# A four-image mixer kernel: first image loaded ahead of the setup, the operands' sums and more weighing on GpSimd, tanh left in PSUM, reciprocals a step later

## The chip, the cores and the metric

The kernel runs on one core of one Trainium2 chip. A core has TensorE (PE, matrix products into PSUM), VectorE (DVE), ScalarE (ACT) and GpSimd (POOL), each with a queue worked off in order, and a queue (SP) that only issues DMAs here. The metric is the device time of one launch in microseconds (us). All arithmetic is float32.

## The reference, cut to what matters

Four layers follow each other on x of shape (4, 128, 64, 64): 4 images, 128 channels, L = 4096 pixels. Each normalises its input in groups of 4 channels (`gn`) and adds its result to it.

```python
x = x + attention(gn(x))      # q, k, v by 128x128 matrices; softmax over all 4096 pixels; no heads
x = x + conv5x5(gn(x), c)     # c is gathered from small tables by index, c = tab_xx[i]*XX + tab_id[i]*identity
x = x + mamba(gn(x))          # below
x = x + conv3x3(gn(x), main_w)

def mamba(x):                 # 64 channels forward, 64 over the reversed pixels
    t  = Wx @ x + bx
    xt = silu(conv1d(t, 4 taps) + conv_b)
    delta = softplus(xt @ Wd + bd);  Bm = xt @ WB;  Cm = xt @ WC        # 64 states
    dA = exp(delta * A);  dBx = delta * xt * Bm;   A = -exp(Alog)
    h[l] = dA[l]*h[l-1] + dBx[l]                                        # for 128 channels x 64 states
    y = sum_over_states(h * Cm) + D * xt
    return Wp @ y + bp
```

## The kernel before

One program is written out by Python generators, so the order on each queue is the order in which these emit.

**The scan** (`scan_core`) is the long part: 128 channels x 64 states x 4096 steps per image, cut into 256 *ticks* of 128 rows (32 channels x 4 states) x 1024 steps, 1024 ticks in all. A chunk of 1024 steps lasts 64 ticks. A tick i is: `drive` on POOL (db = dx * b, L946), two `decay` on ACT (da = exp, into PSUM, L939), `recur` on DVE (the recurrence, two halves of 512, L956), weighing with the c row, either on DVE (L959, da in PSUM is one input) or in `weigh` on POOL (L977, both inputs in SBUF), and every second tick `collect` on PE (the sum over states, L991). `to_pool` (L899) says which: two ticks of five (i % 5 in 1, 3), and every third tick of the last image. In the loop at L1027 tick i emits the drive of i+2, the decay of i+1, recur i, weigh i-1, collect i-3 and the DMA loads of i+4 (`AHEAD`).

**The rest** (`images`, L1162) is emitted between the ticks: after each half tick the main loop (L1225) takes steps from the generator `work` until a credit of 1.4 is used up (`PACE` 2.8 per tick; 0.75 in the last image); a step returns its cost, 0.86 for a product of 512 columns, 0.7 for a `SLOT`. So while image b is scanned, image b+1 goes through attention (`attention`, 256 steps u of a score product, an exp and a value product each), the 5x5 convolution (`conv_pairs`) and the preparation of its scan (`scan_prep`, `scan_operands`). While the last image is scanned, the 3x3 convolutions of the others run. Image 0 has nothing to hide behind: its attention, convolution and half of its operands come before the first tick.

**The operands** (`scan_operands`) are laid out by hand over 51 slots. For tile i of 512 pixels, starting at slot 5i: the taps on PE into PSUM bank `s` (`taps`), in slot 5i+4 two ACT passes (`halves`, L783: half of it to xc; L785: tanh into an SBUF tile th), in slot 5i+5 `silu` on DVE (L789: xc = (th+1)*xc, two SBUF inputs), then three products (bank `a`, `z`, `s2`), softplus on ACT and `digits` on DVE. For each half of the image (HM = 4 tiles) slot 5(i+3)+15 takes the logarithms on ACT (`logs`), and then for each chunk of 1024: `join` (L823, DVE: delta += u, 512 wide, twice, both inputs in SBUF; DMA to `dd`), two slots later `drives` (L828, POOL: xc = delta * xc; DMA to `dxd`). When a half is through, `(b, i + HM)` is put in `ready`; `before(b)` (L1210), called ahead of the first loads of image b's scan, takes steps until the first half is ready.

**Attention's tail**: when block blk of 512 queries is through, `evict` copies acc; one step later `turn` brings the row sums onto the partitions (8 or 4 narrow PE products into bank `z`) and has DVE copy them (L494) and take the reciprocal (L496); two steps after that `settle` spreads the reciprocals (PE, bank `z`, L407) and DVE multiplies and adds (L504 to L506). For image 0 the row sums are gathered beside the attention by side sums of the exponentials (`side_sums`, L466 and L469: even steps DVE, odd POOL); for the others by PE (`sums`, L449, bank `z`).

**The start.** Constants are computed first from `wm` in the pool `early` (L102), which is closed at L205 after the tap weights `wtap` (L196). The pools of the large tiles are opened only in `program` (L1177), on the space that `early` gave back, and the first image is loaded into them. `build_conv_weights` (L218) gathers the 5x5 weights on DVE in 13 steps while image 0's attention begins; after each the main loop takes one step of attention (L1200).

Of the kernel before, what the change touches and what calls it, by code (L numbers as in the profile page):

```python
# [32 lines left out]
P = 128  # L33
# [19 lines left out]
def conv_preact_kernel(  # L53
# [45 lines left out]
    wv = const.tile([P, C], F32, name="wv")  # L99
    nc.scalar.dma_start(wv, mats[:, 2, :])  # L100
    setup = ExitStack()
    early = setup.enter_context(tc.tile_pool(name="early", bufs=1))  # L102
# [20 lines left out]
    def col(i):  # L123
        return vec[:, i : i + 1]
# [12 lines left out]
    a_neg = const.tile([P, NK * NQ], F32, name="a_neg")  # L137
    with tc.tile_pool(name="rates", bufs=1) as tmp:
        every = tmp.tile([P, NK, NQ, NI], F32, name="every")
        for k in range(NK):  # L140
            rates = vecs[k * SG : (k + 1) * SG, ALOG : ALOG + NST].unsqueeze(1)
            nc.scalar.dma_start(
                every[:, k].rearrange("p q j -> p (q j)"),
                rates.to_broadcast([SG, NI, NST]),
            )
        mine = tmp.tile([P, NI], F32, name="mine")
        nc.vector.tensor_reduce(
            mine, ident.rearrange("p (s i) -> p i s", i=NI), AX.X, ALU.add
        )
        every = every.rearrange("p k q i -> p (k q) i")  # L150
        mine = mine.unsqueeze(1).to_broadcast([P, NK * NQ, NI])
        nc.vector.tensor_tensor(every, every, mine, ALU.mult)
        nc.vector.tensor_reduce(a_neg, every, AX.X, ALU.add)
    nc.scalar.activation(a_neg, a_neg, AF.Exp)
    nc.vector.tensor_scalar(a_neg, a_neg, -1.0, None, ALU.mult)

    sel = const.tile([P, SG], F32, name="sel")
    nc.vector.tensor_reduce(
        sel, ident.rearrange("p (s i) -> p s i", i=NI), AX.X, ALU.add
    )  # L160
    skip = const.tile([P, P], F32, name="skip")
    nc.vector.tensor_scalar(skip, ident, col(DSKIP), None, ALU.mult)

# [26 lines left out]
    cbias = small.tile([P, 1], F32, tag="cbias", bufs=1, name="cbias")  # L190
    for k in range(KC):
        ptap = bank("saz"[k % 3], f"ptap{k}")[:, :C]
        nc.tensor.matmul(
            ptap, col(CONVW + k).to_broadcast([P, P]), ident, start=True, stop=True
        )
        nc.vector.tensor_tensor(wtap[:, k, :], wm[:, 3, :], ptap, ALU.mult)  # L196
    for t in range(KC - 1):

        nc.vector.tensor_reduce(
            edge[:, t : t + 1], vec[:, CONVW : CONVW + KC - 1 - t], AX.X, ALU.add  # L200
        )
    nc.vector.tensor_tensor(cbias, edge[:, 0:1], col(CONVW + KC - 1), ALU.add)
    nc.vector.scalar_tensor_tensor(cbias, cbias, col(BX), col(CONVB), ALU.mult, ALU.add)
    nc.vector.tensor_scalar(edge, edge, col(BX), -1.0, ALU.mult, ALU.mult)
    setup.close()  # L205
    hbias = const.tile([P, 1], F32, name="hbias")
    nc.vector.tensor_scalar(hbias, cbias, 0.5, None, ALU.mult)

# [161 lines left out]

    def attention(b, xs, xn, v, st, safe):
        ring = pools["big"].tile([P, NRING, MM], F32, tag="xt", name=f"pt_{b}")
# [107 lines left out]
        def turn(blk):  # L480

            raw, zs = state[blk]
            parts = [(zs, zsel)] if zs is not None else [
                (sides.pop((blk, e)), ones[:, 0:1]) for e in "dp"
            ]
            pz = bank("z", f"pz_{b}_{blk}")
            for t in range(TPM):
                for n, (part, add) in enumerate(parts):
                    nc.tensor.matmul(
                        pz[:, t : t + 1], part[:, bass.ts(t, P)], add,  # L490
                        start=n == 0, stop=n == len(parts) - 1,
                    )
            z = zall[:, b * NJT + blk * TPM : b * NJT + (blk + 1) * TPM]
            nc.vector.tensor_copy(z, pz[:, :TPM])  # L494
            zr = small.tile([P, TPM], F32, tag="zr", name=f"zr_{b}_{blk}")
            nc.vector.reciprocal(zr, z)  # L496
            state[blk] = raw, zr

        def settle(blk):
            raw, zr = state.pop(blk)  # L500
            pb = bank("z", f"pzb_{b}_{blk}")
            spread(pb, zr)
            cut = bass.ts(blk, MM)
            nc.vector.tensor_tensor(pb, raw, pb, ALU.mult)  # L504
            nc.vector.scalar_tensor_tensor(xs[:, cut], pb, bv_c, xs[:, cut], ALU.add, ALU.add)
            nc.vector.bn_stats(st[:, blk, :], xs[:, cut])  # L506
# [5 lines left out]
        for u in range(N + 2):  # L512
# [8 lines left out]
            if 0 <= w < N:  # L521
# [10 lines left out]
                if d == NJT - 1:  # L532
                    evict(blk - 1)
                    if blk < NM:
                        after(u, 1, turn, blk - 1)
                        after(u, 3, settle, blk - 1)
                    else:
                        turn(blk - 1)
                        yield PRODUCT
                        settle(blk - 1)  # L540
                        ready.add((b, "attended"))
                        break
# [3 lines left out]
            for f, args in later.pop(u, ()):  # L546
                f(*args)
                cost += PRODUCT
            yield cost or HOP
# [198 lines left out]
    def scan_operands(b, xn, mats4, piece):  # L748
# [3 lines left out]
        pad = KC - 1  # L752
        HM = NM // 2

# [25 lines left out]
        def halves(i):  # L780

            pt = pts.pop(i)
            nc.scalar.activation(xc[:, bass.ts(i, MM)], pt, AF.Identity, scale=0.5, bias=hbias)  # L783
            ths[i] = pools["bg"].tile([P, MM], F32, tag="w", bufs=4, name=f"th_{b}_{i}")
            nc.scalar.activation(ths[i], pt, AF.Tanh, scale=0.5, bias=hbias)  # L785
# [34 lines left out]
        def join(c):  # L820
            for i in range(c * CH // MM, (c + 1) * CH // MM):
                cut = bass.ts(i, MM)
                nc.vector.tensor_tensor(delta[:, cut], delta[:, cut], us.pop(i), ALU.add)  # L823
            nc.sync.dma_start(dd[c], delta[:, bass.ts(c, CH)])
# [19 lines left out]

        def logs(i):
            for n in range(i, i + HM):
                nc.scalar.activation(us[n], us[n], AF.Ln)
# [7 lines left out]
        for i in range(NM):  # L855
# [12 lines left out]
            at(t + 13, row, i, 2)  # L868
        for i in (0, HM):
            t = EVERY * (i + HM - 1) + 15  # L870
            at(t, logs, i)
            for n, c in enumerate(range(i * MM // CH, (i + HM) * MM // CH)):
                at(t + 1 + n, join, c)
                at(t + 3 + n, drives, c)
            at(t + 3 + HM * MM // CH, ready.add, (b, i + HM))
        at(1, piece, 1)
        at(2, piece, 2)
        at(2, ready.add, (b, "read"))
        at(EVERY * (NM - 1) + 4, ready.add, (b, "taps"))
        for t in range(max(slots) + 1):  # L880
            for f, args in slots.get(t, ()):
                f(*args)
            yield SLOT
        ready.add((b, "all"))

# [3 lines left out]
    def scan_core(mats4, ynds, before, widen, result):  # L889
# [7 lines left out]
        das = {}  # L897

        def to_pool(i):  # L899

            return i % 5 in (1, 3) if ticks[i][0] + 1 < B else i % 3 == 2

# [5 lines left out]
        def load(i):  # L908
            b, c, d, q, g = ticks[i]
            (bmat, cmat), dd, dxd, xcd, _ = mats4[b]  # L910
            if q == 0:
                for name, src in (("de", dd), ("dx", dxd)):
                    t = pools["rep"].tile([P, CH], F32, tag=name, name=f"{name}_{b}_{c}_{d}_{g}")
# [147 lines left out]
    def program(safe):  # L1061
# [22 lines left out]
        def front(b, xn, v):  # L1084

            xs = large(b + 1, f"xs_{b}")[:, :L]
            yield from load(xs, b)
            st = stats_tile(f"e{b}")
            yield from attention(b, xs, xn, v, st, safe)
            st2 = stats_tile(f"s{b}")  # L1090
# [85 lines left out]
        with ExitStack() as es, tc.manual_schedule():  # L1176
            pools["big"] = es.enter_context(tc.tile_pool(name=f"big{safe}", bufs=1))  # L1177
            pools["bg"] = es.enter_context(tc.tile_pool(name=f"bg{safe}", bufs=2))
            banks = ExitStack()
# [15 lines left out]
            if not safe:  # L1195
                with tc.tile_pool(name="fill", bufs=2) as pools["fill"]:
                    while not (0, "begun") in ready:
                        next(work)
                    with tc.tile_pool(name="tables", bufs=1) as tmp:
                        for _ in build_conv_weights(tmp):  # L1200
                            next(work)
                    while (0, "attended") not in ready:
                        next(work)
                del pools["fill"]
            pools["rep"] = es.enter_context(tc.tile_pool(name=f"rep{safe}", bufs=3))
            pools["rows"] = es.enter_context(tc.tile_pool(name=f"rows{safe}", bufs=3))
# [3 lines left out]
            def before(b):  # L1210

                nonlocal pace
                while (b, NM // 2) not in ready:
                    next(work)
# [24 lines left out]

    program(False)  # L1240


# [72 lines left out]
```

## Time and profile before

| | us |
|---|---|
| median of 3 runs | 4618.73 (4616.98 to 4622.92) |
| profiled execution | 4616.38 |
| its span, first to last instruction | 4613.4 |
| ahead of the first tick (first db) | 751.75 |
| image 0's ticks, up to image 1's first db | 986.2 |
| image 1's | 975.2 |
| image 2's | 976.5 |
| image 3's, to its last db | 832.4 |
| from there to the end | 91.3 |

| engine | busy us | share of the span |
|---|---|---|
| PE | 4058.3 | 88% |
| DVE | 3758.6 | 81% |
| POOL | 3561.4 | 77% |
| ACT | 2320.9 | 50% |

Shares of the whole span hide that the stages have different limits, so the profile is read by stretches: of each, how long every engine was busy. The clock granted to TensorE was 0.938 of full speed on the mean.

### The profile page before, as it was taken

The page shows a single profiled execution, that of the slowest core. Times are in us where ns is not written, and L with a number is a line of the kernel's source. Part 1 is how long each engine was busy: PE and PEld are TensorE (multiplying, and loading weights), DVE is VectorE, ACT ScalarE, POOL GpSimd, SP SyncE. Part 2 cuts the span into 40 slices and gives each one's busy share as a digit, 9 for nine tenths or more (in the row PEclk, how much of TensorE's full clock was granted, in tenths as well). Part 3 has the DMA queues.
Part 4 walks back from the last instruction along what each step waited for, and adds up shares of the span by engine and source line. Part 5 has one row for each costly group of instructions (what it writes and reads, how often), then busy time and mean ns, then how long its engine had stood idle before and what let it go on. Part 6 is the DMA issues. An engine that isn't in the chain of part 4 may idle for free. (4 is left out here: it accounts for less than half of the span.)

```text
span 4613.4 us, 43452 instructions
## 1 busy us (share of the span) xinstructions
PE 4058.3 (88%) x13568; PEld 1496.7 (32%) x13568; DVE 3758.6 (81%) x3672; ACT 2320.9 (50%) x4180; POOL 3561.4 (77%) x1684
## 2 busy tenths in 40 slices
PE   6999998999999978999999979999999658585767
PEld 3444443333333323333333333333333112121212
DVE  7222115989998989999999989999999999999993
ACT  2333206666665466666664476666554644444431
POOL 2333304889988968898989869899899699999992
PEclk9999998999999989999999989999999878787878
DMA  1000005454444446445444564544445565656561
GB/s 66 1 0 1 0 18 214 171 166 169 169 171 157 171 182 217 158 170 177 171 167 157 200 219 171 173 174 167 162 163 180 205 233 201 220 206 220 196 228 44
DMA packets 210577, 719.47 MB, mean 156 GB/s; under 512 B 24864, under 2 KB 25760, under 8 KB 210208
## 3 DMA queue, kind: packets, MB, share of 16 engines
q1 hardware_dynamic: 208736, 715.87, 44.3%
q8 instruction: 109, 1.79, 0.2%
q14 instruction: 132, 1.08, 0.1%
q10 hardware_dynamic: 1600, 0.73, 0.1%
HBM read 649.07 MB, written 67.44 MB: 155 GB/s over the span
## 5 line engine op out<-in xcount | busy, mean ns | idle before, releaser
L946 POOL TENSOR_TENSOR db<-dx,br 128x1024 f32<-128x1024 f32 x1024 | 2403.9, 2367 | 339.0 <-DVE hc L956 75.7
L939 ACT ACTIVATE da<-de,a_neg 128x512 f32<-128x512 f32 (+1 forms) x1793 | 1343.5, 752 | 1011.0 <-DVE da L956 690.8
L415 PE MATMUL sc<-r,x 128*128 128x512 f32 x2048 | 1090.3, 615 | 53.5 <-ACT last L972 23.4
L427 PE MATMUL acc<-pt,v 128*128 128x512 f32 x2048 | 1050.1, 595 | 1.7
L977 POOL TENSOR_TENSOR hc<-hc,cr 128x1024 f32<-128x1024 f32 x392 | 929.1, 2370 | 11.4 <-ACT last L972 8.5
L991 PE MATMUL y<-hc,sel 128*32 128x512 f32 x4096 | 674.1, 654 | 279.6 <-POOL hc L977 262.5
L959 DVE TENSOR_TENSOR hc<-da,cr 128x512 f32<-128x512 f32 (+1 forms) x1094 | 847.6, 775 | 70.1 <-DVE da L956 0.5
L421 ACT ACTIVATE pt<-sc 128x512 f32<-128x512 f32 x1024 | 601.6, 588 | 512.9 <-PE sc L415 475.1
L956 DVE TENSOR_TENSOR_SCAN da<-da,last,db 128x512 f32<-128x512 f32 (+1 forms) x474 | 740.7, 1563 | 20.0 <-POOL db L946 13.2
L956 DVE TENSOR_TENSOR_SCAN da<-da,da,db 128x512 f32<-128x512 f32 x462 | 594.5, 1287 | 16.2 <-ACT da L939 15.7
L415 PEld LDWEIGHTS sc<-r,x 128*128 128x128 f32 x2048 | 358.7, 190 | 658.4 <-issue 389.2
L427 PEld LDWEIGHTS acc<-pt,v 128*128 128x128 f32 x2048 | 388.4, 190 | 500.2 <-issue 481.3
L956 DVE TENSOR_TENSOR_SCAN hc<-da,last,db 128x512 f32<-128x512 f32 (+1 forms) x294 | 442.9, 1506 | 2.8 <-POOL db L946 1.4
L956 DVE TENSOR_TENSOR_SCAN hc<-da,hc,db 128x512 f32<-128x512 f32 x307 | 393.9, 1283 | 36.1 <-ACT da L939 4.2
L469 POOL TENSOR_TENSOR sidep<-sidep,pt 128x512 f32<-128x512 f32 x120 | 156.8, 1307 | 313.4 <-ACT pt L421 313.4
L991 PEld LDWEIGHTS y<-hc,sel 128*32 128x32 f32 x4096 | 96.4, 111 | 751.2 <-POOL hc L977 365.7
L581 PE MATMUL pcm<-xpm,cw 128*128 128x512 f32 x576 | 289.8, 651 | 31.7 <-ACT xpm L321 31.7
L469 DVE TENSOR_TENSOR sided<-sided,pt 128x512 f32<-128x512 f32 x120 | 89.3, 744 | 249.6 <-ACT pt L421 248.4
L696 PE MATMUL pe<-df,cw 128*128 128x512 f32 x640 | 289.3, 597 | 0.0
L956 DVE TENSOR_TENSOR_SCAN da<-da,db 128x512 f32<-128x512 f32 (+1 forms) x158 | 236.6, 1498 | 12.0 <-ACT da L939 7.4
L972 ACT COPY last<-da 128x1 f32<-128x1 f32 x473 | 73.8, 156 | 276.7 <-DVE hc L959 274.1
L449 PE MATMUL zp<-pt,ones 128*32 128x512 f32 x1536 | 208.9, 595 | 0.0
(178 smaller groups left out, 2685.7 us busy)
## 6 DMA issues: line engine op xcount, KB each, us to landing
br<-bm SPq DMA_DIRECT2D x512, 512.0 KB, 5.1
cr<-cm SPq DMA_DIRECT2D x512, 512.0 KB, 4.0
de<-dd SPq DMA_DIRECT2D x64, 512.0 KB, 4.7
dx<-dxd SPq DMA_DIRECT2D x64, 512.0 KB, 6.1
x<-in_x_dram SPq DMA_DIRECT2D x16, 512.0 KB, 5.3
xs<-in_x_dram SPq DMA_DIRECT2D x16, 512.0 KB, 5.9
xsd<-xs SPq DMA_DIRECT2D x16, 512.0 KB, 5.5
xcd<-xc SPq DMA_DIRECT2D x16, 512.0 KB, 2.7
```

Of the source, the lines that this page charges most:

```text
L415: nc.tensor.matmul(sc, xn[:, bass.ts(j, P)], rq[blk], start=True, stop=True)
L421: nc.scalar.activation(pt, sc, AF.Exp)
L427: nc.tensor.matmul(acc[blk], v[:, j, :], ring[:, u % NRING, :], start=j == 0, stop=j == NJT - 1)
L469: eng.tensor_tensor(s, s, ring[:, u % NRING, :], ALU.add)
L581: nc.tensor.matmul(acc.rearrange("p (r w) -> p r w", w=W), weights[:, t, :], xp[:, y : y + RPM, dx : dx + W], start=t == 0, stop=t == k * ...
L696: nc.tensor.matmul(flat(acc), cw[:, w * K5 + dx, :], view(r, dx), start=k == 1, stop=k == total and (n == 0 or not lean),)
L939: nc.scalar.activation(da, rep["de", b, c, d, g][:, bass.ts(h, size)], AF.Exp, scale=a_neg[:, at(i)])
L946: nc.gpsimd.tensor_tensor(dbs[i], rep["dx", b, c, d, g], rows["b", b, c, d, q], ALU.mult)
L956: nc.vector.tensor_tensor_scan(h, da, db[:, cut], before, ALU.mult, ALU.add)
L959: nc.vector.tensor_tensor(hc[:, cut], h, rows["c", b, c, d, q][:, cut], ALU.mult)
L977: nc.gpsimd.tensor_tensor(hcs[i], hcs[i], rows["c", b, c, d, q], ALU.mult)
L991: nc.tensor.matmul(y[r : r + SG, :], sel, hcs[i - KG + 1 + gg][:, bass.ts(h, MM)], start=q == 0, stop=False, tile_position=(0, r), skip_gr ...
```

## The change

1. The pools `big` and `bg` are opened ahead of `early`, so the first image's tile does not lie on the space of `early`.
2. The tap weights, edges, biases and rates that only the scan needs move from the setup into a generator `scan_constants`. It runs ahead of `build_conv_weights`, beside image 0's attention, and after each step of either four steps of attention are taken instead of one.
3. The second copy of each image (`xs`) is loaded one chunk per step of attention, not all ahead of it.
4. `turn` keeps the products; copy and reciprocal (`invert`) come a step later; the spreading (`widen_out`) in step 4 and the multiplication (`settle`) in step 5, where both were in step 3.
5. For images 1 to 3 tanh is written over its input in PSUM.
6. `join` is on POOL.
7. The operands of image 0 become ready in three parts (1, 2 and 1 chunks), the others' in two as before; the scan's first loads wait for the first part only.
8. While operands are being emitted, three ticks of five are weighed on POOL instead of two; not in the last image.

```diff
+    lower = ExitStack()
+    pools["big"] = lower.enter_context(tc.tile_pool(name="big", bufs=1))
+    pools["bg"] = lower.enter_context(tc.tile_pool(name="bg", bufs=2))
     setup = ExitStack()
     early = setup.enter_context(tc.tile_pool(name="early", bufs=1))
...
+    def scan_constants():
+        for k in range(KC):
+            ptap = bank("z", f"ptap{k}")[:, :C]
...
+            yield HOP
+            nc.vector.tensor_tensor(wtap[:, k, :], wm[:, 3, :], ptap, ALU.mult)
...
+            state[blk] = raw, pz
+
+        def invert(blk):
+            raw, pz = state[blk]
             z = zall[:, b * NJT + blk * TPM : b * NJT + (blk + 1) * TPM]
             nc.vector.tensor_copy(z, pz[:, :TPM])
...
-                        after(u, 1, turn, blk - 1)
-                        after(u, 3, settle, blk - 1)
+                        for n, f in ((1, turn), (2, invert), (4, widen_out), (5, settle)):
+                            after(u, n, f, blk - 1)
...
+            next(loads, None)
             yield cost or HOP
...
-            ths[i] = pools["bg"].tile([P, MM], F32, tag="w", bufs=4, name=f"th_{b}_{i}")
+            ths[i] = pt if b > 0 else pools["bg"].tile(
+                [P, MM], F32, tag="w", bufs=4, name=f"th_{b}_{i}"
+            )
             nc.scalar.activation(ths[i], pt, AF.Tanh, scale=0.5, bias=hbias)
...
-                nc.vector.tensor_tensor(delta[:, cut], delta[:, cut], us.pop(i), ALU.add)
+                nc.gpsimd.tensor_tensor(delta[:, cut], delta[:, cut], us.pop(i), ALU.add)
...
-        for i in (0, HM):
-            t = EVERY * (i + HM - 1) + 15
-            at(t, logs, i)
+        cuts = (0, PER, NM - PER, NM) if b == 0 else (0, NM // 2, NM)
+        for i, j in zip(cuts, cuts[1:]):
+            t = EVERY * (j - 1) + 15
+            at(t, logs, i, j)
...
+                at(t + 4 + n, ready.add, (b, "operands", c))
...
-            return i % 5 in (1, 3) if ticks[i][0] + 1 < B else i % 3 == 2
+                pooled[i] = (
+                    i % 3 == 2 if ticks[i][0] + 1 == B
+                    else n % 2 == 0 if "operands" in ready else n % 2 == 1
+                )
...
-                        for _ in build_conv_weights(tmp):
-                            next(work)
+                        for _ in chain(scan_constants(), build_conv_weights(tmp)):
+                            for _ in range(4):
+                                next(work)
...
-                while (b, NM // 2) not in ready:
+                while (b, "operands", 0) not in ready:
                     next(work)
```

## The prediction

> **What bounds the kernel now.** I read it by stretches first: busy time of every engine between the events that divide the run (first score, end of the weight gathering, convolution, taps, first db and so on). Columns: stretch, its length, then us busy of PE, weight loads, DVE, ACT, POOL.
>
> ```profile
> 0.00:39.60 39.60, 14.05 (x81) 12.26 (x81) 18.63 (x51) 11.32 (x15) 2.75 (x14) 1.00 0.50 177
> 39.60:115.70 76.10, 61.77 (x127) 25.40 (x128) 64.46 (x52) 19.25 (x33) 23.96 (x15) 0.91 0.02 8
> 115.70:543.30 427.60, 415.31 (x1105) 193.69 (x1103) 100.91 (x162) 143.82 (x240) 139.42 (x119) 0.99 0.00 0
> ...
> 690.50:751.70 61.20, 54.21 (x183) 18.61 (x184) 25.05 (x43) 43.57 (x69) 5.80 (x4) 0.95 0.50 181
> ...
> 1640.00:1805.00 165.00, 124.82 (x468) 47.18 (x472) 145.50 (x163) 110.44 (x187) 113.18 (x54) 0.88 0.58 212
> 1805.00:2612.00 807.00, 785.77 (x2834) 286.55 (x2827) 753.30 (x776) 459.68 (x902) 736.19 (x328) 1.00 0.49 168
> 2612.00:2781.00 169.00, 133.55 (x491) 48.26 (x493) 148.70 (x171) 115.85 (x195) 120.29 (x56) 0.90 0.59 214
> ...
> 3578.00:3745.00 167.00, 104.48 (x353) 27.72 (x353) 155.79 (x140) 99.03 (x156) 125.99 (x57) 0.76 0.64 228
> 3745.00:4522.00 777.00, 527.04 (x1569) 147.41 (x1567) 753.88 (x456) 338.49 (x485) 740.27 (x337) 0.80 0.59 208
> ```
>
> There are five kinds of stretch. To 39.6 nothing is busy. From 39.6 to 115.7 PE waits for DVE. Then PE alone works, 97% of the time. In a scan's middle (1805 to 2612) PE is full (97%) with DVE at 93%. At the three boundaries between images, where operands are made, PE falls to 76, 79 and 63% and DVE is the fullest, with 19.5, 20.3 and 11.2 us idle. The last stretch is DVE's and POOL's. 16 ticks last 53 to 60 us in most of a scan (counted at the db rows), but the last 16 of images 0, 1 and 2 take 91, 91 and 92: that is the boundary.
>
> Next, who waited for whom until 540 us, and the timeline of the start:
>
> ```profile
> PE pv L348 <- ACT x L321: 14.6, 1, 14.6
> PE sc L415 <- ACT pt L421: 11.0, 3, 5.5
> ```
> ```profile
> 14.14 0.29 DVE L196 TENSOR_TENSOR wtap<-wm,ptap 128x128 f32<-128x128 f32 x1 [0.89 <-PE ptap L193]
> 14.51 1.82 SPq L1069 DMA_DIRECT2D x<-in_x_dram  x4
> ...
> 27.44 2.37 ACT L321 ACTIVATE x<-x,nb_a,rs_a 128x1024 f32<-128x1024 f32 x2 [17.36 <-POOL nb_a L316]
> ```
>
> The load of x goes out 0.1 us after the last reader of `wm`: it waits for that space. Last, DVE and POOL side by side at the first boundary, and the groups of the two DVE operations that change:
>
> ```profile
> 1745.01 8.93 DVE L823 TENSOR_TENSOR delta<-delta,u 128x512 f32<-128x512 f32 x4
> ```
> ```profile
> 1745.00 8.39 POOL L946 TENSOR_TENSOR db<-dx,br 128x1024 f32<-128x1024 f32 x3 [2.35 <-DMA dx<-dxd]
> ```
> ```profile
> L823 DVE TENSOR_TENSOR delta<-delta,u 128x512 f32<-128x512 f32 x32 | 43.6, 1414 | 5.3 <-ACT u L847 5.3
> L789 DVE SCALAR_TENSOR_TENSOR xc<-th,xc 128x512 f32<-128x512 f32 x32 | 41.8, 1306 | 36.6 <-ACT th L785 36.6
> L469 POOL TENSOR_TENSOR sidep<-sidep,pt 128x512 f32<-128x512 f32 x120 | 156.8, 1307 | 313.4 <-ACT pt L421 313.4
> ```
>
> Four additions take 8.93 us beside three db, though the median of an L823 is 684 ns (longest 2868). DVE operations with two SBUF inputs stand until the POOL operation ends; L959, whose da is in PSUM, keeps its 692 ns beside the same POOL work.
>
> **1. The start (parts 1, 2).** x is issued at 14.51 and normalised from 27.44, 12.9 us later; scores follow 12.1 us after that. In the changed order x is first on SP, with nothing to wait for, at about 0.7. Its 2 MB now share the engines with some 0.73 MB that ran alone between 2 and 8 us; about 3 MB moved in 16 to 24 us at 0.4 MB per us, so add up to 1.9. Normalising starts near 15.2 (0.7 + 12.9 + 1.6): **-12**. Ends: -8 if the small loads ahead of it, `ssm` on POOL and `wm` on DVE, come late, -14 without sharing.
>
> **2. The weights (part 2).** A step of attention takes 1.72 us on PE; half a block of 16 takes 29.4 to 30.2 once the weights are done, but the first two took 34.5 and 41.6. That is 76.1 - 59.6 = 16.5 us too much. A gathering step holds DVE for 0.17 + 1.82 + 1.82 = 3.8 us, and now four steps of attention (6.9 us, with two side sums of 0.74 on DVE) come to each: 5.3 of 6.9. The ring of 8 exponentials gives 6 steps of slack, so PE should not wait. Cover lost: if a side sum is late at a block's end, PE waits up to 3.8 for it. The moved constants (some 4 us of DVE, 4 products of 0.3) vanish in DVE's 327 idle us. **-15.5** (-10 to -16.5).
>
> **3. Image 0's operands (parts 6, 7).** Five slots last 6.55 us (L789 rows at 710.3, 716.9, 723.4, 730.0). The first drives move from slot 33 to 23: 10 x 1.31 = 13.1 us. What the remaining slots cost then lies beside ticks, where before DVE idled 36 and POOL 55 of 61 us. Against it: one more group of logarithms, two table loads of 1.28 on ACT, hidden (ACT idle 17.6); and two additions at 1.31 on POOL for 0.69 on DVE in the path, +1.2. The work now done beside ticks is repaid by three ticks: in the two programs' orders the convolution and operands of images 1 to 3 stand 2 to 4 ticks later, so when PE's part is over, 3 ticks of about 3.25 us fewer are left. That is the same gain seen from PE, so I count it once: **-13** (-4 to -18).
>
> **4. The three boundaries (parts 5, 6, 8).** Off DVE at each: the additions 11.9, 7.6 and 16.7; the waiting of L789, 13.0, 12.5 and 10.8 less 8 x 0.69, so 7.5, 7.0 and 5.3; and 4 weighs (406 against 392 in the two orders: 4, 5, 4 at the boundaries, 1 elsewhere net) of 1.4 us: 5.5. Sum 25, 20, 27. Onto POOL: 8 x 1.31 + 4 x 2.37 = 20 us where it has 51.8, 48.7 and 41.0 idle. The join now stands in POOL's queue ahead of db two ticks on; if the logarithms are late, those db wait.
>
> The price is part 5. The bank `s` is free for the next taps after silu on DVE, no longer after tanh on ACT. Before, PE started them 0.05 us after tanh ended in most tiles, so that bank is already what PE waits for; but it had products to do (2.93 us) meanwhile. From the end of tanh to the end of silu the first boundary shows 0.7, 1.3, 0.7, 2.6, 3.8, 5.8, 11.8, 6.3 us. Lower end: only 0.7 per tile, mostly hidden. Upper end: all of it, some 25 us, as much as DVE gains. But those lags are DVE's backlog, made of what leaves it. With backlog gone a tile needs 3.65 (taps) + 1.3 (halves) + 0.7 + some 3.5 of queues = 9.2 us; DVE needs 9.0 (two ticks of 2 x 1.28 + 0.4 x 1.38, silu, digits, statistics of the next image), so neither is far ahead. I take about half of what leaves DVE: **-11, -10, -15 = -36** (from -68 to +10).
>
> Two rules of the Trainium skill speak against part 6. GPSIMD Engine Reference, section Engine selection: an elementwise operation with two inputs is about twice as slow there, so VectorE is to have it; Perfetto Trace Analysis, section Optimizing Scalar/DVE Operations, adds that the two share an SBUF read port, so moving work between them might not help. The rows agree with the factor (1307 against 684). By the rules the 24 joins are worth 24 x (0.68 - 1.31), a loss of 15, instead of the 36 us that they hold DVE. The rows decide: where they run, DVE has no idle and POOL has 40 to 50, and most of DVE's time in them is not the addition but the wait for POOL. By the rules the 72 us of this step shrink to 72 - 36 - 15 = 21, half of it -10; by the rows it is -36. What speaks for the rules stays as rival A.
>
> **5. Reciprocals (part 4).** DVE waits 2.4 us a block for the products:
>
> ```profile
> DVE zall L494 <- PE pz L489: 18.9, 8, 3.7
> ```
>
> But there PE is the fuller engine (19 idle of 623 us), and its named waits come to 12 us, mostly for ACT. Bank `z` is held two steps longer; the next sums come due one step after `settle`. Nothing gained below a few us, and PE would stand if DVE were over 2 us behind. **-2** (-10 to +8). Part 3 changes no engine's work: the orders show the eight chunk loads at the same place but for one; 0.
>
> **Sum:** -12 - 15.5 - 13 - 36 - 2 = -78.5. The profiled execution took 4616.4 (span 4613.4 and 3.0 around it), the median of the runs 2.3 more; 4618.7 - 78.5 = **4540**.
>
> **Rivals.**
> A. *POOL takes over at the boundaries* (the rule): its 20 us fall into the 60 us (1700 to 1760) where it has 37 busy and additions, drives and new db come together; the boundaries give nothing. 4540 + 36 = 4576. For: DMA waits of 9 us there stay. Against: 40 idle us.
> B. *DVE was all there was to it*: the boundaries give all 72 but for some latency, 4 us: 4540 - 32 = 4508. Against: PE's wait for silu.
> C. *Slower: the tap bank.* If PE's wait for silu delays taps, products, ACT and the scan's decays in a circle, what leaves DVE only becomes idle time, and silu's lag is added in full. Steps 1, 2, 3 and 5 still give 42.5. It turns the sign from 42.5 / 24 = 1.8 us a tile; at the lags seen (33, 31 and 18 us for the three images) it is 4618.7 - 42.5 + 82 = 4658. For: the lags. Against: they are backlog that is taken away.
> D. *The start gives half*: late small loads or side sums that hold PE, +14: 4554, inside the forecast's range.
>
> **Chances.** Forecast 0.57 (4518 to 4562), A 0.19, B 0.15, D 0.05, C 0.04. For 8 in 10 I reach from B's far side to past A, and take in the loss of a few us at each boundary: 4498 to 4586. A measurement of this kernel tells some 0.2% (9 us) from no change. Faster 0.94, within it 0.02, slower 0.04.
>
> **What would show it.** Step 1: ACT's first normalisation near 15 instead of 27.4. Step 2: half blocks of 30 us from the first. Step 3: first db near 710 (751.7 - 12 - 15.5 - 13). Step 4: last 16 ticks of images 0 to 2 in about 80 instead of 91; L813 (silu) at 0.69 on PSUM; PE waits at the taps with DVE as the releaser, 1 to 2 us each. If the taps wait over 3 us each, or POOL is over 95% there, step 4 is wrong.

## The result and the profile after

| | before | after |
|---|---|---|
| median of 4 runs, us | 4619.75 (4616.98 to 4622.92) | 4558.21 (4557.13 to 4560.34) |
| ratio, with its 95% interval | | 0.9867 (0.985 to 0.9884) |
| span of the profiled execution | 4613.4 | 4555.3 |

The change gains 61.5 us; the forecast was 78.5. The total is near, but its terms are not: one gained 28 us more than it was given, one lost 12 to 24 us where it was to gain 36, and in part these cancel. One execution of the version with parts 5, 6 and 8 undone took 14728 us at a granted clock of 0.455, and that version's figures below are of its three others.

The stretches show where the time went. Below are those of the kernel after: stretch, length, then us busy (and instructions) of PE, weight loads, DVE, ACT and POOL, granted clock, DMA share, GB/s. The ends are events that both kernels have: first score, end of the first two half blocks, first product of the convolution, first taps, first db, next image's first score, last db. The last row alone begins at no such event; it starts 3.8 us ahead of the first product of `scan_end`, at which the table further down cuts.

```profile
0.00:28.80 28.80, 12.15 (x74) 11.02 (x74) 7.84 (x23) 11.07 (x14) 2.75 (x14) 1.00 0.71 244
28.80:84.80 56.00, 55.19 (x132) 24.55 (x133) 17.52 (x39) 19.92 (x34) 19.81 (x15) 1.00 0.00 1
84.80:512.40 427.60, 415.34 (x1105) 193.69 (x1103) 169.47 (x203) 143.81 (x241) 153.83 (x119) 0.99 0.01 2
659.60:704.30 44.70, 41.59 (x144) 13.77 (x144) 14.46 (x22) 30.64 (x48) 4.83 (x3) 0.96 0.52 180
1607.50:1716.30 108.80, 81.87 (x314) 31.46 (x314) 74.82 (x89) 79.58 (x131) 75.17 (x39) 0.87 0.59 210
1716.30:2375.00 658.70, 643.36 (x2434) 235.15 (x2434) 615.05 (x636) 409.82 (x837) 606.15 (x266) 1.00 0.50 175
...
3675.10:4460.70 785.60, 532.80 (x1588) 151.24 (x1588) 759.40 (x461) 342.24 (x492) 745.94 (x340) 0.80 0.59 208
```

For two of them the same stretch of the kernel before, cut at the same events (operands of image 1 up to image 2's first score; image 2's attention):

```profile
1651.60:1763.50 111.90, 83.36 (x322) 31.77 (x322) 98.38 (x107) 81.15 (x131) 70.15 (x32) 0.88 0.58 207
1763.50:2428.30 664.80, 645.02 (x2434) 234.93 (x2435) 615.56 (x637) 408.24 (x837) 597.79 (x262) 1.00 0.49 170
```

To read: the first two half blocks took 76.1 us, now 56.0 with PE busy for 55.2 of them. The first tick comes 44.7 us after the taps, not 61.2. At the boundary DVE is busy for 74.8 us instead of 98.4, nearly as much off it as the prediction worked out (25), and the stretch is only 3 us shorter, with three ticks fewer in it: most of the time has turned into idle time. Image 2's attention is shorter by 6.1, though no engine's work there falls by more than 1.7.

All stretches, in us, with the ticks (db rows) that ran in them:

| stretch | before | after | difference |
|---|---|---|---|
| start, to the first score | 39.6 | 28.8 | -10.8 |
| attention of image 0 | 503.8 | 483.6 | -20.2 |
| its operands, to the next first score | 90.1, 7 ticks | 92.8, 8 | +2.7 |
| attention of images 1, 2, 3 | 673.9, 664.8, 665.4; 550 ticks | 659.1, 658.7, 658.3; 555 | -28.0 |
| operands of images 1, 2, 3 (of image 3 to the first product of `scan_end`) | 111.9, 108.8, 132.1; 62 ticks | 108.9, 115.8, 140.8; 61 | +12.7 |
| from there to the last db | 796.0, 245 ticks | 781.8, 240 | -14.2 |

The convolutions and the end after the last db changed by 1.2 us or less each. The last 16 ticks of images 0, 1 and 2, which the prediction wanted in about 80 us instead of 91, 91 and 92, take 90, 92 and 87.

The start went nearly as expected: the first normalisation, in the timeline of ACT after, with the time since the instruction before it and the releaser in brackets:

```profile
16.50 2.37 ACT L331 ACTIVATE x<-x,nb_a,rs_a 128x1024 f32<-128x1024 f32 x2 [5.43 <-POOL nb_a L326]
```

It is at 16.5 instead of 27.4.

At the first boundary (1607 to 1717) the waits of the kernel after: engine, line and releaser, then us in all, times, longest.

```profile
PE pt L790 <- DVE xc L813: 12.8, 5, 6.7
PE pt L790 <- ACT xn L331: 6.4, 1, 6.4
...
DVE hc L995 <- ACT da L978: 13.4, 8, 4.1
DVE pb L841 <- ACT u L867: 9.4, 5, 5.3
DVE xc L813 <- ACT pt L809: 8.8, 4, 3.8
...
POOL delta L847 <- ACT u L871: 10.2, 1, 10.2
...
ACT bs L827 <- PE pb L822: 17.1, 5, 9.6
```

Each of the engines shown waits for another. PE waits at the taps (L790) for `silu` (L813), ACT waits for PE's products (L822), and DVE stands for 31.6 us for ACT: for the decays (L978), for softplus (L867) and for tanh (L809). The timeline has the longest of them; PE, POOL, DVE and ACT follow each other here, each with start, duration, idle time before and releaser:

```profile
1671.39 6.60 PE L790 MATMUL pt<-xn,wtap 128*64 128x512 f32 x16 [6.70 <-DVE xc L813]
...
1657.42 4.95 POOL L847 TENSOR_TENSOR delta<-delta,u 128x512 f32<-128x512 f32 x4 [10.22 <-ACT u L871]
...
1662.08 0.70 DVE L841 SCALAR_TENSOR_TENSOR pb<-u,pb 128x512 f32<-128x512 f32 x1 [5.32 <-ACT u L867]
...
1670.68 0.65 DVE L813 SCALAR_TENSOR_TENSOR xc<-pt,xc 128x512 f32<-128x512 f32 x1
...
1662.99 0.67 ACT L809 ACTIVATE pt<-pt,hbias 128x512 f32<-128x512 f32 x1
...
1679.08 0.58 ACT L827 COPY bs<-pb 128x512 f32<-128x512 f32 x1 [9.55 <-PE pb L822]
```

tanh of this tile is through at 1663.66. `silu` starts at 1670.68, behind two recurrences and the statistics of the next image's normalisation, which are ahead of it on DVE. Until then the bank is held, PE waits 6.70 us for it, and ACT waits 9.55 us for the products that stand behind the taps. Before the change the bank was free when tanh was through, and PE's waits at the taps in the same stretch (image 1's operands) were small:

```profile
PE pt L769 <- ACT th L785: 2.9, 4, 1.1
```

`silu` itself takes 0.65 to 0.69 as the prediction said: its price is right, its place isn't.

### The profile page after: what moved, and what is told of

Same layout as the page of the kernel before. It is cut to its first block, busy times and chain, and to the rows that moved or that the text cites. A ratio compares the mean times of both kernels' runs of the same rounds, so it can differ in the third digit from the quotient of the medians.

```text
span 4555.3 us, 43425 instructions
## 1 busy us (share of the span) xinstructions
PE 4028.3 (88%) x13568; PEld 1492.3 (33%) x13568; DVE 3698.8 (81%) x3615; ACT 2322.5 (51%) x4184; POOL 3633.0 (80%) x1730
## 3 DMA queue, kind: packets, MB, share of 16 engines
q1 hardware_dynamic: 208736, 715.87, 44.7%
## 5 line engine op out<-in xcount | busy, mean ns | idle before, releaser
L978 ACT ACTIVATE da<-de,a_neg 128x512 f32<-128x512 f32 (+1 forms) x1795 | 1344.2, 752 | 889.0 <-DVE da L995 553.0
L426 PE MATMUL sc<-r,x 128*128 128x512 f32 x2048 | 1080.9, 610 | 21.2 <-ACT r L395 12.8
L1016 POOL TENSOR_TENSOR hc<-hc,cr 128x1024 f32<-128x1024 f32 x406 | 960.1, 2365 | 13.5 <-ACT last L1011 10.4
L998 DVE TENSOR_TENSOR hc<-da,cr 128x512 f32<-128x512 f32 (+1 forms) x1067 | 828.4, 776 | 67.8 <-issue 0.4
L995 DVE TENSOR_TENSOR_SCAN da<-da,last,db 128x512 f32<-128x512 f32 (+1 forms) x464 | 727.9, 1569 | 23.2 <-POOL db L985 16.9
L995 DVE TENSOR_TENSOR_SCAN da<-da,da,db 128x512 f32<-128x512 f32 x449 | 577.8, 1287 | 11.5 <-ACT da L978 10.5
L995 DVE TENSOR_TENSOR_SCAN hc<-da,last,db 128x512 f32<-128x512 f32 (+1 forms) x304 | 455.7, 1499 | 6.6 <-ACT da L978 2.7
L995 DVE TENSOR_TENSOR_SCAN hc<-da,hc,db 128x512 f32<-128x512 f32 x322 | 413.1, 1283 | 57.9 <-ACT da L978 27.2
L480 POOL TENSOR_TENSOR sidep<-sidep,pt 128x512 f32<-128x512 f32 x120 | 167.4, 1395 | 283.7 <-ACT pt L432 281.4
```

The costliest lines, as they stand in the source:

```text
L426: nc.tensor.matmul(sc, xn[:, bass.ts(j, P)], rq[blk], start=True, stop=True)
L480: eng.tensor_tensor(s, s, ring[:, u % NRING, :], ALU.add)
L978: nc.scalar.activation(da, rep["de", b, c, d, g][:, bass.ts(h, size)], AF.Exp, scale=a_neg[:, at(i)])
L995: nc.vector.tensor_tensor_scan(h, da, db[:, cut], before, ALU.mult, ALU.add)
L998: nc.vector.tensor_tensor(hc[:, cut], h, rows["c", b, c, d, q][:, cut], ALU.mult)
L1016: nc.gpsimd.tensor_tensor(hcs[i], hcs[i], rows["c", b, c, d, q], ALU.mult)
```

## The experiments

Each run keeps the changed kernel but for the edit shown. A part's worth is the difference between the run's ratio to before and 0.9867, times 4619 us; ratios have intervals of about 0.0017 to either side (8 us), so a difference of less than some 10 us isn't told from none unless the stretches agree. A stretch is measured in one execution of each version.

### Tanh in PSUM undone (part 5)

```diff
-            ths[i] = pt if b > 0 else pools["bg"].tile(
-                [P, MM], F32, tag="w", bufs=4, name=f"th_{b}_{i}"
-            )
+            ths[i] = pools["bg"].tile([P, MM], F32, tag="w", bufs=4, name=f"th_{b}_{i}")
```

> The changed kernel with tanh in an SBUF tile again for all images (part 5 undone, all else kept). Changed kernel: 4558 us, span 4555.3; its three boundaries (taps to next image's first score) take 108.9, 115.8, 136.9 us, with PE waiting 12.8 us at the first one for silu on DVE. Theory T (tap bank): PE's wait for silu is what ate the boundary gain; without it the three boundaries shrink by some 8 us each although silu waits for POOL again, total 4530 to 4540. Rival P (POOL's queue): the additions and their wait for the logarithms block db; the tap bank is beside the point and silu's return to two SBUF inputs costs 5 us a boundary: 4565 to 4575. Rival F (forced emission ahead of an image's scan): no change beyond 5 us either way.

Measured 4541.35 us, ratio 0.9833 (0.9817 to 0.985): part 5 costs 16 us. The boundaries of images 1 and 2 shorten by 6.1 and 7.7 us, that of image 3 by 0.4. The waits of the first boundary (PE):

```profile
PE pt L790 <- ACT xn L331: 6.7, 1, 6.7
...
PE pt L790 <- ACT th L807: 3.5, 4, 1.4
```

The wait for `silu` of 12.8 us is gone; that for tanh, which takes its place, is 3.5. That `silu` again has two SBUF inputs costs less than the lock. The boundaries that gain are those with one long wait of the taps for `silu` (6.70 us at image 1, 11.24 at image 2); at image 3 the longest is 1.4, and nothing is gained there.

### The join back on DVE (part 6)

```diff
-                nc.gpsimd.tensor_tensor(delta[:, cut], delta[:, cut], us.pop(i), ALU.add)
+                nc.vector.tensor_tensor(delta[:, cut], delta[:, cut], us.pop(i), ALU.add)
```

> The changed kernel with the join additions on DVE again (part 6 undone, all else kept). Theory T: the additions gave DVE 25 us a boundary that became idle time, so undoing them costs little at the boundaries, 0 to 10 us in all: 4558 to 4568. Rival P: POOL no longer stands 10 us for the logarithms in front of db, gain of 15 to 25 us: 4533 to 4543. As predicted before (additions worth about half of what they hold DVE): loss of 18 us and more, 4576.

Measured 4547.27, ratio 0.9842 (0.9826 to 0.9859): part 6 costs 11 to 12 us. The stretches agree: attention of images 1 to 3 is shorter by 5.0, 5.0 and 2.7, their operands change by +0.8, -1.9 and +2.8. Of the 5.0 us at image 1, 1.9 are there by the eighth of its 512 score products and 3.9 by the 192nd. Where the gain comes from is not shown. The additions on POOL wait in order for the logarithms (10.22 us above), and what is behind them on POOL waits too; but with the additions on DVE, POOL stands as long at the product behind them, in the same boundary:

```profile
POOL xc L852 <- PE pt L790: 11.4, 1, 11.4
```

So this wait is there either way and can't be what the part costs.

### The extra weighing on POOL undone (part 8)

```diff
-                    else n % 2 == 0 if "operands" in ready else n % 2 == 1
+                    else n % 2 == 1
```

> The changed kernel with two ticks of five on POOL throughout (part 8 undone). As DVE is idle 34 us in each boundary of the changed kernel, 4 weighs of 1.4 us returned to DVE cost nothing under T, and POOL gets 10 us back: 4553 to 4560. If DVE bound the boundaries, as predicted before, +8: 4566. Rival P: POOL's relief gains 10 to 20: 4540 to 4548.

Measured 4556.57, ratio 0.9863 (0.9847 to 0.988): no difference. Weighing four ticks more on DVE costs nothing that can be measured while DVE is idle, in this run too, for 27 to 31 us of a boundary.

### Parts 5 and 6 undone, and with them part 8

The first run makes the first two edits above together, the second all three.

> The changed kernel with tanh in SBUF and the join on DVE (parts 5 and 6 undone together). Alone, undoing part 5 gave -17 us and part 6 -11. Theory Q (both were waits put into an engine's queue: PE's for silu, POOL's for the logarithms; they are separate): the two add up, -24 to -30, near 4531. Rival M (each undoing only moves the same idle time, the other then covers it): no better than part 5 alone, 4538 to 4545. Rival V (DVE becomes full again, with 25 us more a boundary on it): worse than either, 4550 and above.

Measured 4535.58, ratio 0.9815 (0.9798 to 0.9831): 24 us faster than the change, a little under the sum of both (27).

> tanh in SBUF, join on DVE, and two of five ticks weighed on POOL throughout: all of step 4 (parts 5, 6, 8) undone, the rest of the change kept. Theory N (step 4 as a whole is a net loss because what it takes off DVE at the boundaries becomes DVE idle): 20 to 30 us faster than the changed kernel, 4530 to 4540, as the run with parts 5 and 6 undone (4535.6) since part 8 alone moved nothing. Theory S (part 8 is worth nothing only because parts 5 and 6 have emptied DVE; without them DVE is the bound again and part 8 counts): 5 to 15 us slower than the run with parts 5 and 6 undone, 4541 to 4551. The prediction's step 4 (-36): 4594.

Measured 4539.48 (the middle of three runs, 4535.99 to 4546.78), ratio 0.984 (0.9821 to 0.986), with a span of 4534.1. It can't be told from the run with part 8 kept, so whether part 8 has a worth of its own here stays open; what the run settles is that the prediction's step for the boundaries, forecast at 4594 without them, has the wrong sign. Its stretch of image 1's operands, and PE's waits in it:

```profile
1608.30:1707.90 99.60, 78.64 (x315) 30.54 (x315) 89.22 (x105) 80.32 (x131) 65.40 (x30) 0.92 0.67 229
```
```profile
PE pt L790 <- ACT xn L331: 6.4, 1, 6.4
PE pt L790 <- ACT th L807: 2.7, 3, 1.4
```

DVE does 14.4 us more than after the change, POOL 9.8 less, and the stretch is 9.2 us shorter, with one tick more in it. (At images 2 and 3 the operands take 7.1 us less and 2.8 more.)

### Copy and reciprocal at once again (part 4)

```diff
-                        for n, f in ((1, turn), (2, invert), (4, widen_out), (5, settle)):
+                        for n, f in ((1, turn), (1, invert), (3, widen_out), (3, settle)):
```

> The changed kernel with copy, reciprocal, spreading and settling at the old steps 1 and 3 (part 4 undone). The attention stages of images 1 to 3 went from 673.9, 664.8, 665.4 us to 659.1, 658.7, 658.3 with 5 ticks more in them. Theory R: that is the reciprocal's later step, DVE no longer stands 2.4 us a block for PE; undone, the stages return to 665 or more and the time to 4590 (+30). Rival S: it comes from elsewhere (the placing of loads, the shift of three ticks); undone, the time stays within 5 us, as the prediction of -2 us for this part had it.

Measured 4588.03, ratio 0.9932 (0.9915 to 0.9948): part 4 is worth 30 us, half of the whole gain. Attention of images 1 to 3 is longer by 7.5, 11.3 and 9.7, nothing else changes by more than 2.4. Image 2's attention, waits of DVE, ACT and PE, first after the change:

```profile
DVE zall L509 <- PE pz L500: 1.7, 1, 1.7
...
ACT da L978 <- DVE da L995: 91.3, 74, 3.9
...
PE sc L426 <- ACT last L1011: 2.5, 2, 1.7
```

and with part 4 undone:

```profile
DVE zall L509 <- PE pz L500: 15.8, 6, 3.4
...
ACT da L978 <- DVE da L995: 126.0, 79, 5.1
...
PE sc L426 <- ACT last L1011: 8.0, 7, 2.4
```

Read from the top: DVE stands for the row sums' products (15.8 us a stretch), the recurrences behind them are late, so the decay, which writes the bank that a recurrence frees, keeps ACT waiting (126.0 instead of 91.3; ACT's wait for score products falls meanwhile, from 94.7 to 65.0). Behind it on ACT's queue are the exponentials of attention, and PE's score products wait for what ACT hasn't reached. DVE's idle time grows by 11.4 us (43.6 to 55.0), PE's by 7.1 (15.3 to 22.4), the stretch by 11.3. That the wait passes through ACT's order is read from these rows; no run takes ACT's part out of it alone. Nor does the run part the later reciprocal from the later multiplication; but DVE's wait for the spread reciprocals (L523) is 2.5 us after the change and 2.8 here, so the wait that goes is that at L509.

### One step of attention for a gathering step (part 2)

```diff
-                            for _ in range(4):
-                                next(work)
+                            next(work)
```

> The changed kernel with one step of attention after each step of the constants and weights, as before the change, not four. Image 0's attention took 503.8 us before and 483.6 in the changed kernel. If the spacing of the gathering is the cause, this run's takes 500 or more (the moved constants add to the pile) and the time is +16 to +24: 4574 to 4582. Rival: moving x's load and the constants was what freed PE; then within 5 us of the changed kernel.

Measured 4586.86, ratio 0.9932 (0.9915 to 0.9948); image 0's attention is 511.6 instead of 483.6. PE's waits from 28 to 120 us:

```profile
PE sc L426 <- ACT pt L432: 17.6, 5, 5.5
```

After the change this line isn't there. The spacing is what gains. Waits are not all of the 28.0 us: from 60 to 120 us the granted clock is 0.83 in this run, where after the change it is 1.00 up to 84.8, so PE's own work takes longer too. The 28.0 us are more than the change's 20.2; the constants moved out of the setup, which now stand in the same place, may be the reason, but no run shows it apart.

### The early part of image 0 undone (the cut of part 7)

```diff
-        cuts = (0, PER, NM - PER, NM) if b == 0 else (0, NM // 2, NM)
+        cuts = (0, NM // 2, NM)
```

> The changed kernel with image 0's operands ready in two halves, as all other images' (the cut of part 7 undone; the readiness by chunk is kept, both chunks of a half come at once). The prediction gave the earlier first tick 13 us, counted once with the three ticks by which all later work stands later. If right: +13, 4571. Theory F (the three ticks also push the operands of images 1 to 3 against the stop ahead of the next image's scan, where no tick is emitted meanwhile): the first tick comes 16 us later but most is paid back there, +0 to +6: 4558 to 4564.

Measured 4560.49, ratio 0.9878 (0.9861 to 0.9894): 2 us slower by the medians, 5 by the ratios, neither told from none. The early start is given back. Without it the operands of image 1 take 8.1 us more and the last stretch 7.6, with 243 ticks instead of 240; but image 0's operands take 4.4 less, the attention of images 2 and 3 2.9 and 5.7 less, and image 2's operands 2.1 less: 15.7 against 15.1.

### The copy's loads ahead of attention (part 3)

```diff
-            yield from attention(b, xs, xn, v, st, safe, load(xs, b))
+            yield from load(xs, b)
+            yield from attention(b, xs, xn, v, st, safe, iter(()))
```

> the second copy of each image is loaded ahead of attention, as before the change (part 3 undone), the rest as changed. Theory 0 (part 3 changes no engine's work): 4553 to 4563, no difference from the changed kernel. Theory X (the loads of eight chunks at once stand in SP's queue ahead of the scan's loads and delay a few ticks per image): 5 to 15 us slower, 4563 to 4573.

Measured 4563.55, ratio 0.9884 (0.9867 to 0.99): 5 to 8 us slower, within the two intervals. The stretches that differ most are attention of images 1 and 2 (+2.3, +1.7). It is not settled.

### The pace of the background work

The steps taken for a tick set how many ticks are through when PE's work ends. Three runs change it, first 2.84 with part 5 undone, then 2.76 and 2.72 with parts 5 and 6 undone:

```diff
-PRODUCT, HOP, SLOT, PACE, ENDPACE, AHEAD = 0.86, 1.7, 0.7, 2.8, 1.5, 4
+PRODUCT, HOP, SLOT, PACE, ENDPACE, AHEAD = 0.86, 1.7, 0.7, 2.76, 1.5, 4
```

> As e1_no_psum_tanh (tanh in SBUF, 4541.4 us), and 2.84 of work per tick instead of 2.8, so that the operands of images 1 to 3 come 4, 6 and 9 ticks earlier and nothing is forced out ahead of an image's scan. Theory F: the stop where no tick is emitted (POOL waits 10 us for the logarithms, DVE 5 us) goes at each of three boundaries: -10 to -20, 4522 to 4532. Rival: the stop is no loss, as PE has the same products to do in it; PE's total is unchanged: within 4 us of 4541. Against it: more work a tick lengthens the middle, and fewer ticks are done when PE is through with image 3, 9 x 3.25 = 29 us more to do in the last stretch, less what PE gained in time: up to +10.

4564.96, ratio 0.9881 (0.9864 to 0.9897), 22 us slower than 2.8. The last stretch has 258 ticks instead of 240 and takes 835.9 us instead of 783.6; the operands of image 3 are only 18.8 shorter.

> parts 5 and 6 undone, and PACE 2.76 in place of 2.8. Theory G (while PE is the bound, fewer steps to a tick mean that more ticks are done when PE is through; 2.84 cost 23.6 us in the other direction): about 1.4% more ticks beside PE's work, some 7 to 8 ticks of 3.25 us fewer at the end, 10 to 25 us faster than the run with parts 5 and 6 undone: 4511 to 4526. Theory H (2.8 stands at the best point: DVE, which has 93% in the scan's middle, becomes the bound and PE waits for the scan): the attention stages lengthen by as much or more, 4536 to 4560.

4525.20, ratio 0.9802 (0.9786 to 0.9819). The last stretch has 3 ticks fewer and is 9.7 us shorter, and the operands of the three images are 3.4, 7.7 and 10.1 shorter; attention of image 1 is 8.0 longer, with 3 ticks more. The gain over 2.8 is 10 us by the medians, inside both intervals, so it is likely but not shown. Against the changed kernel it is: the intervals (to 0.9819, from 0.985) don't meet. It is the fastest version run.

> as before with PACE 2.72. Theory G: twice the gain, 4490 to 4515. Theory H: slower than 2.8, 4545 to 4580. If 2.76 gains and 2.72 does not, the point at which DVE takes over lies between.

4545.45, ratio 0.9846 (0.9829 to 0.9862), slower than 2.76. Attention of images 1 to 3 is 14.5, 13.4 and 6.9 longer than at 2.8, for 16 ticks more. In the first of these DVE is busy 633.5 us instead of 619.4, 95% of the stretch both times: the length grew as DVE's work did, by 2.2 and 2.3%, though PE's work grew as well (636.9 to 648.3). That 2.72 is too low is shown, since its interval doesn't meet that of 2.76; which of 2.76 and 2.8 is the better is not.

## Why the prediction was right in total and wrong in its terms

| term | predicted | measured | from |
|---|---|---|---|
| 1 start | -12 | -10.8 | stretches |
| 2 weights | -15.5 | -20.2 | stretches; the run with one step to one shows the cause |
| 3 first operands | -13 | -2 to -5, not told from 0 | run with one cut fewer |
| 4 boundaries | -36 | +12 to +24, a loss | runs with parts 5, 6, 8 undone |
| 5 reciprocals | -2 | -30 | run with part 4 undone |
| part 3 | 0 | 0 to -8, not told from 0 | run with loads ahead |

That the total came out within 17 us of the forecast is luck in good part: the boundaries missed by 48 to 60 us one way, the first operands by 8 to 11 the same way, and the reciprocals by 28 the other.

Added up, the terms reach from -39 to -62, and the measured -61.5 lies at the end of that. By the spans of the profiled executions some 10 us are left that no run undid alone; the earlier end of the forced steps ahead of a scan (part 7, images 1 to 3) was not tried. That is open.

**The start** was right but for 1.2 us.

**The weights.** The cause was right, the size short: I set the two half blocks against 59.6 us, two of the later ones. PE lost more than that, since the first half block has two value products fewer and no block's tail ahead of it: 26.6 us after the change. The loss was 76.1 - 56.0 = 20.1. Of this 6.6 us are PE's own busy time (61.8 to 55.2, with the granted clock at 0.91 before and 1.00 after), which the prediction had not set apart.

**The first operands.** The first tick came at 704.3, near the 710 of the forecast, and it gained 16.5 us against the taps. The sum took it as final, "so I count it once", and there the step failed: it is a loan. Without the early part the first tick comes 16.3 us later, and the time is the same within what can be told. The work put beside ticks makes these longer (the first 16 took 76.0 us instead of 66.5), and the stretches of that run have the rest of it come back in the attention of images 2 and 3, where PE and DVE are both nearly full. The three ticks fewer at the end did come: 240 instead of that run's 243.

**The boundaries** are the failed step. "I take about half of what leaves DVE" had the amounts right (98.4 - 74.8 = 23.6 against the 25 worked out for the first) and the bound wrong. I had found that DVE was the fullest engine there (13.5 us idle of the 111.9), and took a full engine for the limit. What the waits of the stage show is a circle through in-order queues: taps, ACT's halves and tanh, `silu`, products, softplus. The runs test one link of it: part 5 made the circle tighter, at 16 us. Over the three images the taps wait 36.1 us for `silu`, where before they waited 8.6 for tanh. What part 6 adds (11 to 12 us) stays without a shown cause. My point of failure was set at "over 3 us each". The mean is 36.1 / 24 = 1.5, below it; the harm is done by one tile each of images 1 and 2 (6.70 and 11.24 us). A threshold on a mean is blind to that. The sign of rival C's mechanism ("what leaves DVE only becomes idle time") was right, and its price, 82 us, far too high, so its time of 4658 was off by 100.

**Part 6 against the rule.** I set aside what the Trainium skill says against it (GPSIMD Engine Reference, section Engine selection), since the trace had DVE standing for POOL in these additions. The twofold duration holds (1271 ns on POOL, 1414 with its waits or 684 without on DVE), and the rule's answer, leave it, was the right one: the move costs 11 to 12 us, near the loss of 15 that the prediction worked out from the two durations and then set aside. Whether the longer duration is also the reason is not shown: POOL has 33.6 us idle in the first boundary after the change.

**The reciprocals** are the other failed step. "There PE is the fuller engine", and so DVE's 18.9 us of waiting seemed hidden. PE was busy for 97%, but the largest of its named waits there is on ACT, whose queue stood behind DVE. A wait on an engine that isn't the fullest can count; by the rows, it does so here where ACT's in-order queue carries it on. Of the 14.1 us of waiting at L509 that part 4 removes from image 2's attention, 11.3 come out as time. The price I put at "nothing gained below a few us" was the whole of it.

**The rivals.** The time lies halfway between the forecast (4540) and A (4576), which had the boundaries give nothing. POOL didn't take over: it is busy 75.2 us of 108.8 there. B, everything gained, is excluded by the result.

## What to carry to other kernels

Before crediting time taken off a full engine, ask for the *chain* that the stage runs along: where queues are worked off in order and buffers are one deep, the fullest engine need not be the limit, and its freed time can show up as idle, as here. Releasing a PSUM bank earlier was worth more here than a shorter instruction, as the next work waited for the bank; so write over a bank's content only if its reader is near. Where an engine that is not full waits, ask who stands behind it in the next engine's queue.

## What the hardware showed

The taps that followed the 6.70 us wait took 6.60 us instead of 3.65. Granted clock (the eighth figure of a row) around them, after the change:

```profile
1655.00:1658.70 3.70, 3.65 (x16) 1.05 (x16) 1.76 (x3) 3.67 (x6) 1.28 (x2) 1.00 0.35 144
1671.40:1674.70 3.30, 3.30 (x8) 1.00 (x10) 3.23 (x4) 0.00 (x0) 3.23 (x3) 0.50 0.92 304
1674.70:1678.00 3.30, 3.30 (x11) 0.80 (x7) 2.97 (x4) 0.00 (x0) 3.30 (x2) 0.60 0.43 170
1678.00:1680.80 2.80, 2.80 (x10) 0.92 (x10) 0.51 (x1) 1.72 (x4) 0.60 (x1) 1.00 0.10 37
```

TensorE ran at about half its clock for some 6 us and then at full again. After 11.24 us at the second boundary the same 16 products took 5.88, and after waits of 1.33 to 2.12 in this kernel they took 3.65:

```profile
2638.80 5.88 PE L790 MATMUL pt<-xn,wtap 128*64 128x512 f32 x16 [11.24 <-DVE xc L813]
```

That is in keeping with the Trainium skill (TensorE: Matmul & The Clock Gate, section Why this matters for your kernels), which has a gap of over some 3 us end at half rate. But the length of the one wait doesn't settle it here: in the kernel before, 16 products of the taps took 5.26 us after a wait of 2.57, at a granted clock of 0.69, with two shorter waits just ahead of it. After the change the lower clock adds 2.2 and 3.0 us to the two long waits, so a lock of the tap bank costs more than its wait.

On DVE an addition with two SBUF inputs took up to 2868 ns beside POOL in the kernel before, and `silu` 1306 in the mean. With one input in PSUM `silu` takes 685 (24 of them). That saves 0.6 us a tile, some 15 us of DVE's time over the 24 tiles, and the lock that goes with it is dearer: part 5 costs 16 us with this saving counted.
